# Two chained cross-attentions: the semantic product in 32-row tiles, with the Gram matrix's symmetry between token groups

## The chip, the cores and the metric

One core of a Trainium2 chip runs the kernel. Its engines are TensorE (PE in the profile, with PEld for its weight loads), VectorE (DVE), ScalarE (ACT), GpSimd (POOL) and SyncE (SP), whose queue issues nearly all DMAs here. The metric is the device time of one execution in microseconds (us). Each engine works through its own instructions in order; semaphores hold an instruction back until its inputs are there.

## The reference

64 batch elements of 256 queries and 320 channels, with a context of 77 tokens of 512 channels, pass through two cross-attentions, 20 heads of 16 channels each. The first layer is plain softmax attention over the 77 tokens (its image branch over an empty set of tokens gives nothing). The second, cut to what matters:

```python
text_ehs, ip_ehs = encoder_hidden_states[:, :-4], encoder_hidden_states[:, -4:]   # 73 and 4 tokens
probs_t = softmax(einsum('bhsd,bhtd->bhst', q, k_t) * attn_scale)
text_out = einsum('bhst,bhtd->bhsd', probs_t, v_t)
attn_scores = einsum('bhsd,bhnd->bhsn', q, k_ip) * attn_scale
qsem = l2norm(einsum('bhst,bte->bhse', probs_t, text_ehs))     # 512 channels, per head and query
sem = einsum('bhse,bne->bhsn', qsem, l2norm(ip_ehs))
probs_ip = softmax(attn_scores + 0.5 * sem) * spatial_mask
out = (text_out + einsum('bhsn,bhnd->bhsd', probs_ip, v_ip)) @ W_out + b_out + residual
```

`qsem` need not be built. With the Gram matrix G = ctx ctx^T of the 77 tokens, the dot product of an unnormalized qsem with an image token is the weight vector w times a column of G, and its squared norm is w^T G w. So one product of w with a matrix [G | values | ones] of 77 + 16 + 1 = 94 columns (GV) gives, per head and query: 73 columns whose weighted sum is the norm, 4 image scores, the 16 channels of the text output and the softmax's sum. This is the semantic product.

## The kernel before, in words

The batch is worked in pairs of elements (p, 32 pairs). A pair has ten units per layer (u = 0 to 4 for b = 0, then for b = 1); a unit is 128 rows of queries times 8 heads, laid out as 4 row quarters r by 2 heads e. The main loop has one step g per unit; step k = g mod 10 of a pair runs unit g of the first layer and, 13 steps later (LAG), the same unit of the second layer. Within a step PE runs, in this order: the semantic product of the second layer's unit of two steps ago (`semantics`), both layers' scores (`scores`, L659) into the same PSUM tile `sc`, the transposes of the second layer's weights (`transposed`, L723, L724), some of the projections, and the transposes of the first layer's. `sc` has one set of four banks, one for each quarter r, so the next step's product can begin only when DVE and ACT have read this one: DVE takes the maxima (`mx`, L677), subtracts (`w`, L679), multiplies the semantic columns with the weights (`weighted`, L792 and L795, into `prod`) and reduces them to the norm (`nrm`, L1130); ACT copies the 21 other columns out (`sums`, L1057). ACT takes the exponentials: L690 writes the first 64 tokens of a second-layer unit into `parts1` and L691 the other 9; both are turned by PE and copied by ACT to `pt1` and `pr1` (L730, L731). POOL normalizes the first layer's weights (`parts`, L710).

The 73 tokens are split into 64 (M) and a rest of 9 (R1). Two heads' 64 tokens stand on the 128 rows of `pt`: chunk i, half j. The product of the 64 takes tiles of 64 rows by 64 columns of the array; the rest of all eight heads stands on one chunk of 128 rows, 32 per quarter, in tiles of 32 rows by 64, and adds to 30 columns (GR) of each head (L781):

```python
for i in range(4):
    for j in range(2):                       # 64 rows of pt: one head's 64 tokens
        for c in halves_of(P):               # 64 queries
            matmul(ps[c, i % 2 * 2 + j, at : at + GV], pt[half_rows, i, c], gv[b][half_rows, part, i, :], ...)   # L774
```

What the product multiplies with lies in `gv` (the 64) and `gr` (the 9), once for each b. `gram` (L512 to L527; in step k = 0 for b = 0 of the pair before, in k = 5 for b = 1) computes G; ACT copies it out (L516, L517), POOL scales the columns (L518 to L520: image columns by the norms, the columns of the 9 by 2, since their transposed part is left out), SP copies the 64 rows to the lower half of the partitions (L521) and the 9 rows to eight places of `g_rest` (L525). `place_gram` (k = 1 and 8) lets POOL spread them into `gv` (L530) and `gr` (L534). The values of both layers come from `value_rows` (k = 6 and 8), which writes them to DRAM (`v_rows`, L394). `values` (k = 0 and 4 for the second layer, 9 and 2 for the first) loads them back (L406): the 64 rows twice into `vm`, the rest eight times into `vr` or `v_rest`; `place_values` (k = 2 and 8; first layer 0 and 3) puts them into `gv` (L435, L441) and `gr` (L449, L455) on POOL. `keys_by_head` (L376, POOL) spreads the keys into `kbd`, which the scores multiply with; those of the second layer's b = 0 follow `place_gram` in step k = 1 and are first used in step k = 3.

PE, ACT, DVE and POOL run in the order in which the program issues their instructions (`keep_order`). For SP the scheduler chooses, after the first steps: a DMA can be issued ahead of ones that the program names before it. A DMA that waits holds all that stand behind it on SP.

## Time and profile before

| what | value |
|---|---|
| time, median of 3 runs | 2474.22 us (2473.43 to 2474.65) |
| the profiled execution's own time | 2474.45 us |
| its span, first to last instruction | 2472.7 us |
| TensorE clock granted | 0.999 of full |
| from one semantic product to the next in the chain, 1026 to 1100 us | 6.0 to 9.0 us |
| DVE waits for scores (mx after L659) | 339.3 us, 221 times |
| PE waits for ACT sums before the product (L774) | 23.0 us in the page's group |
| mean DMA traffic | 53 GB/s, 150914 packets |

How to read it: an engine's busy share says little here, since records of PE overlap each other. A line of a group gives line, engine, operation, tiles written and read, shape and count, then busy time, mean time of one, and idle time before it with what ended it. In the timeline a line gives the start in us from the span's start, the length, and how many records are merged in it. A shape such as 64*64 is the part of PE's array in use (rows by columns), and 64x94 the moving operand (rows by columns).

### The profile page before, as it was taken

Reading aid. Unit: us, or ns where it says so; the run is one execution under the profiler, and the core shown is the slowest. Engines: PE = TensorE matmul, PEld = TensorE weight load, DVE = VectorE, ACT = ScalarE, POOL = GpSimd, SP = SyncE. Lnnn points to the kernel's source line nnn. Section 1 sums busy time; section 2 is a strip of 40 time slices with the busy share of each in tenths; the row PEclk is TensorE's granted clock in tenths of the full one; section 3 lists DMA queues with packets and bytes.
Section 4 is the critical chain, followed back from the end, with each engine's and each line's share of the span. In section 5 each row is a group of like instructions: output and inputs, shape, how many; then the busy total and the mean of one; then the engine's idle time right before and its main releaser. Section 6 shows DMA issues by size and latency. Waiting matters only on the chain.

```text
span 2472.7 us, 100470 instructions
## 1 busy us (share of the span) xinstructions
PE 2394.2 (97%) x41118; PEld 1847.9 (75%) x41118; DVE 1987.4 (80%) x3673; ACT 1482.2 (60%) x3767; POOL 1370.9 (55%) x3483
## 2 busy tenths in 40 slices
PE   7899999999999999999999999999999999999888
PEld 5677777777777777777777777777777777777676
DVE  3588788888888888888888888888888888888864
ACT  3466666666666666666665666665665666666543
POOL 2455565566555656555656555556555556555542
PEclk9999999999999999999999999999999999999999
DMA  6212111112111112111121211121211121211000
GB/s 173 75 30 57 50 52 47 56 53 58 52 57 41 54 54 59 52 52 51 47 59 56 62 45 48 46 60 56 62 44 48 47 59 56 61 39 39 26 23 25
DMA packets 150914, 131.83 MB, mean 53 GB/s; under 512 B 45432, under 2 KB 129144, under 8 KB 150456
## 3 DMA queue, kind: packets, MB, share of 16 engines
q1 hardware_dynamic: 149592, 124.27, 17.5%
q8 instruction: 325, 5.32, 0.9%
q10 hardware_dynamic: 864, 1.15, 0.2%
q14 instruction: 133, 1.09, 0.1%
HBM read 87.43 MB, written 33.91 MB: 49 GB/s over the span
## 4 chain that ended last, share of the span: by engine, by line
PE 76%; DVE 12%; ACT 3%; DMA 3%; POOL 2%; issue 1%; SPq 1%; DVEq 0%; POOLq 0%; ACTq 0%
PE tr L723 10%; PE sc L774 9%; PE o_ps L547 8%; PE q_ps L547 8%; PE sc L659 7%; DVE w L679 5%; PE v_ps L390 4%; PE sc L781 4%; PE o_ps L632 3%; DVE mx L677 3%; PE k_ps L345 3%; PE pv L809 2%; PE q_ps L557 2%; PE o_ps L557 2%; PE q_ps L575 2%; PE pv L814 2%
## 5 line engine op out<-in xcount | busy, mean ns | idle before, releaser
L677 DVE TENSOR_REDUCE mx<-sc 128x8 f32<-128x584 f32 (+1 forms) x640 | 496.6, 776 | 342.1 <-PE sc L659 339.3
L710 POOL TENSOR_TENSOR parts<-w,sm 128x512 f32<-128x512 f32 (+1 forms) x640 | 440.6, 709 | 437.1 <-DVE sm L706 144.2
L679 DVE TENSOR_TENSOR w<-sc,mx 128x616 f32<-128x616 f32 x640 | 511.8, 800 | 73.0 <-DVE mx L677 1.4
L723 PE MATMUL tr<-ident,parts 128*128 128x128 f32 x2560 | 407.5, 282 | 9.5 <-ACT pt L730 5.6
L730 ACT COPY pt<-tr 128x512 f32<-128x512 f32 x320 | 187.1, 585 | 323.8 <-PE tr L723 318.9
L723 PEld LDWEIGHTS tr<-ident,parts 128*128 128x128 f32 x2560 | 284.2, 140 | 128.6 <-issue 83.1
L687 ACT ACTIVATE w<-w 128x616 f32<-128x616 f32 x320 | 230.1, 719 | 143.7 <-DVE w L679 142.7
L774 PEld LDWEIGHTS sc<-gv,pt 64*64 64x64 f32 x10240 | 233.5, 133 | 105.6 <-ACT sums L1057 52.7
L774 PE MATMUL sc<-gv,pt 64*64 64x94 f32 x10240 | 277.9, 245 | 23.6 <-ACT sums L1057 23.0
L694 POOL COPY att<-w 128x32 f32<-128x32 f32 x320 | 67.0, 209 | 354.6 <-DVE w L679 350.8
L705 DVE TENSOR_REDUCE sm<-w 128x8 f32<-128x616 f32 x320 | 250.9, 784 | 13.9 <-ACT w L687 13.8
L659 PE MATMUL sc<-kbd,q 32*64 32x154 f32 x10240 | 247.7, 293 | 1.1 <-ACT q L602 1.0
L547 PE MATMUL q_ps<-x,wq 128*128 128x256 f32 x1024 | 232.9, 380 | 5.3 <-ACT kT L348 5.3
L547 PE MATMUL o_ps<-aT,wo 128*128 128x256 f32 x1024 | 231.8, 379 | 0.7 <-ACT aT L945 0.7
L1057 ACT COPY sums<-sc 128x168 f32<-128x168 f32 x320 | 96.2, 301 | 225.8 <-DVE prod L795 223.9
L1130 DVE TENSOR_REDUCE nrm<-prod 128x8 f32<-128x584 f32 x320 | 226.7, 709 | 0.3
L792 DVE TENSOR_TENSOR prod<-sc,parts 128x512 f32<-128x512 f32 x320 | 217.9, 681 | 2.8 <-PE sc L781 2.8
L547 PEld LDWEIGHTS q_ps<-x,wq 128*128 128x128 f32 x1024 | 189.2, 190 | 30.2 <-ACT kT L348 7.3
L547 PEld LDWEIGHTS o_ps<-aT,wo 128*128 128x128 f32 x1024 | 189.6, 190 | 24.4 <-ACT aT L945 1.1
L690 ACT ACTIVATE parts<-w 128x512 f32<-128x512 f32 x320 | 206.4, 645 | 0.0
L749 ACT COPY pt<-tr 128x512 f32<-128x512 f32 x256 | 150.3, 587 | 66.9 <-PE tr L723 65.5
L390 PE MATMUL v_ps<-wv,cf 128*128 128x320 f32 (+1 forms) x624 | 179.2, 433 | 0.0
(144 smaller groups left out, 4560.3 us busy)
## 6 DMA issues: line engine op xcount, KB each, us to landing
out_dram<-x SPq DMA_DIRECT2D x64, 256.0 KB
x<-in_x_dram SPq DMA_DIRECT2D x31, 512.0 KB
v_rows<-vs SPq DMA_DIRECT2D x38, 320.0 KB
vm<-v_rows SPq DMA_DIRECT2D x152, 80.0 KB
ct<-in_ctx_dram SPq DMA_DIRECT2D x32, 308.0 KB
cf<-in_ctx_dram SPq DMA_DIRECT2D x38, 256.0 KB
g_rest<-gram_rest SPq DMA_DIRECT2D x512, 0.5 KB
v_rest<-v_rows SPq DMA_DIRECT2D x448, 11.2 KB
```

The lines of the kernel that those rows point to most:

```text
L390: nc.tensor.matmul(ps[:n, :C], cfs[i][:, k, :n], wv[l][:, k, :], start=(k == 0), stop=(k == KE - 1))
L547: nc.tensor.matmul(ps[b][:, m, :], w[:, k, m * P : (m + 1) * P], main[:, k, b * S : (b + 1) * S], start=(k == 0 and m == 0), stop=False,)
L659: nc.tensor.matmul(ps[c, r, 2 * T * l : 2 * T * (l + 1)], tokens[rows, c], kbd[rows, part].rearrange("p e t -> p (e t)"), start=start, sto ...
L677: nc.vector.tensor_reduce(mx, sc[:, :, :, :nt], AX.X, ALU.max)
L679: nc.vector.tensor_tensor(w, sc, mx.unsqueeze(3).broadcast_to([P, 4, 2, T]), ALU.subtract)
L687: nc.scalar.activation(w, w, AF.Exp, scale=SCALE)
L705: nc.vector.tensor_reduce(sm, w, AX.X, ALU.add)
L710: nc.gpsimd.tensor_tensor(two[:, 8 * t0 : 8 * t1].rearrange("p (h t) -> p h t", h=8), w[:, :, t0:t1], sm.unsqueeze(2).broadcast_to([P, 8, ...
L723: nc.tensor.transpose(ps[:, i, :], flat[:, i * P : (i + 1) * P], ident)
L774: nc.tensor.matmul(ps[c, i % 2 * 2 + j, at : at + GV], pt[half_rows, i, c], gv[b][half_rows, part, i, :], start=start and i < 2, stop=False,)
L792: nc.vector.tensor_tensor(prod[:, :, :, :M], sm[:, :, :, :M], w[:, :4].rearrange("p (e a) j t -> p (a j) e t", e=2), ALU.mult)
L1130: nc.vector.tensor_reduce(eight(stats[q, b][2], u), prod, AX.X, ALU.add)
```

## The change

The 64 main tokens are split into two groups of 32 (h = 0, 1), so that the token groups are 32, 32 and 9. The weights are written in the order (e, h) by (r, t): each chunk i is one head e and one group h, with the four quarters r on 32 rows each. The product of the 64 then takes tiles of 32 rows by 64 columns, like the rest and the scores. For h = 0 it computes all 94 columns; for h = 1 only the 62 from the second group on, as the Gram matrix is symmetric: the block of the first group's rows and the second's columns is doubled (a new POOL instruction in `gram`), and its transposed block is left out, as is done with the rest already. `gv` holds, for each row quarter, only that quarter's heads. The Gram rows go to the four quarters by eight DMAs into a new tile `gq` instead of one; the second layer's values are loaded sorted by row quarter (runs of 32 channels), for which `v_rows` gets a copy of its last 64 channels, written by one more DMA; `place_values` is then two POOL instructions instead of 14, and `place_gram` two copies (one for each h) and the same product for the rest. The first layer's values are loaded as before, but `vm` and the new `vq` no longer share a buffer. PE, ACT, DVE and POOL keep their order otherwise; of SP's DMAs, one g_rest comes first, then the eight gq, then the other seven g_rest.

```diff
-    gv = [const.tile([P, 3, 4, GV], F32, tag=f"gv{b}", name=f"gv{b}") for b in range(2)]
+    gv = [const.tile([P, 2, 3, 2, GV], F32, tag=f"gv{b}", name=f"gv{b}") for b in range(2)]
     gr = [const.tile([P, 3, 2, GR], F32, tag=f"gr{b}", name=f"gr{b}") for b in range(2)]
     for b in range(2):
-        nc.vector.memset(gv[b][:, :, :, GV - 1 :], 1.0)
+        nc.vector.memset(gv[b].rearrange("p h i e n -> p (h i e) n")[:, :, GV - 1 :], 1.0)
         nc.vector.memset(gr[b], 0.0)
         nc.gpsimd.tensor_copy(
             gr[b][:, :, :, GR - 1 :], rest1.unsqueeze(1).unsqueeze(3).broadcast_to([P, 3, 2, 1])
...
     for t in vips:
         nc.vector.memset(t[HT * NIP :], 0.0)
-    v_rest = [const.tile([P, C], F32, tag=f"v_rest{b}", name=f"v_rest{b}") for b in range(2)]
+    gq = [const.tile([P, 2, T], F32, tag=f"gq{b}", name=f"gq{b}") for b in range(2)]
+    v_rest = [const.tile([P, 3, QR], F32, tag=f"v_rest{b}", name=f"v_rest{b}") for b in range(2)]
     g_rest = [const.tile([P, R0], F32, tag=f"g_rest{b}", name=f"g_rest{b}") for b in range(2)]
     for t in (*v_rest, *g_rest):
         nc.vector.memset(t, 0.0)
-    parts1 = [const.tile([P, 5, 2, M], F32, tag=f"parts1{i}", name=f"parts1{i}") for i in range(3)]
+    parts1 = [const.tile([P, 5, P], F32, tag=f"parts1{i}", name=f"parts1{i}") for i in range(3)]
     for t in parts1:
         nc.vector.memset(t[:, 4], 0.0)
...
             nc.tensor.matmul(ps[:n, :C], cfs[i][:, k, :n], wv[l][:, k, :], start=(k == 0), stop=(k == KE - 1))
         nc.scalar.copy(stage[i][:n, l, :], ps[:n, :C])
         if l:
-            v_rows[i] = dram.tile([P, 2, C], F32, tag="v_rows", name=f"v_rows{i}", bufs=8)
-            nc.sync.dma_start(v_rows[i][:n], stage[i][:n])
+            v_rows[i] = dram.tile([P, C + 3 * P], F32, tag="v_rows", name=f"v_rows{i}", bufs=8)
+            nc.sync.dma_start(v_rows[i][:n, : 2 * C], stage[i][:n].rearrange("p l c -> p (l c)"))
+            nc.sync.dma_start(v_rows[i][:n, 2 * C :], stage[i][:n, 1, 2 * P :])
             if (i + 2) * P < NB * T:
                 load_rows(i + 2)
-    def from_rows(to, l, p, b, t0, t1):
+    def pieces(p, b, t0, t1):
         r0 = (2 * p + b) * T
         at, end = r0 + t0, r0 + t1
         while at < end:
             i, r = divmod(at, P)
             n = min(P - r, end - at)
-            o = at - r0 - t0
-            nc.sync.dma_start(to[o : o + n, :], v_rows[i][r : r + n, l, :])
+            yield at - r0 - t0, n, v_rows[i][r : r + n]
             at += n
     v0s = {}
...
     def values(l, p, b):
-        nt = (T, TT)[l]
-        rem = nt - M
-        vm = small.tile([P, C], F32, tag="vm", name=f"vm{l}_{p}_{b}", bufs=1)
-        vr = v_rest[b] if l else small.tile([8 * rem, C], F32, tag="vr", name=f"vr{p}_{b}", bufs=1)
-        for e in range(2):
-            from_rows(vm[e * M : (e + 1) * M, :], l, p, b, 0, M)
-        for i in range(8):
-            r = i // 2 * QR + i % 2 * rem if l else i * rem
-            from_rows(vr[r : r + rem, :], l, p, b, M, nt)
+        if l:
+            vm = small.tile([P, 2, 3, QR], F32, tag="vq", name=f"vq{p}_{b}", bufs=1)
+            vr = v_rest[b]
+            by_quarter = lambda rows: rows[:, C:].rearrange("t (i r c) -> r t i c", i=3, r=4)
+            for h in range(2):
+                for o, n, rows in pieces(p, b, h * QR, (h + 1) * QR):
+                    for r in range(4):
+                        nc.sync.dma_start(vm[r * QR + o : r * QR + o + n, h], by_quarter(rows)[r])
+            for o, n, rows in pieces(p, b, M, TT):
+                for r in range(4):
+                    for e in range(2):
+                        at = r * QR + e * R1 + o
+                        nc.sync.dma_start(vr[at : at + n], by_quarter(rows)[r])
+        else:
+            vm = small.tile([P, C], F32, tag="vm", name=f"vm{l}_{p}_{b}", bufs=1)
+            vr = small.tile([8 * R0, C], F32, tag="vr", name=f"vr{p}_{b}", bufs=1)
+            for t0, t1, to, m, count in ((0, M, vm, M, 2), (M, T, vr, R0, 8)):
+                for i in range(count):
+                    for o, n, rows in pieces(p, b, t0, t1):
+                        nc.sync.dma_start(to[i * m + o : i * m + o + n, :], rows[:, :C])
         fetched[l] = (vm, vr)
     def place_values(l, p, b):
...
         rem = (T, TT)[l] - M
         vm, vr = fetched[l]
         if l:
-
-            for j in range(2):
-                rows = slice(j * M, (j + 1) * M)
-                for part in range(2):
-                    nc.gpsimd.tensor_copy(
-                        gv[b][rows, part, :, T : T + D].rearrange("p (e a) d -> p e a d", e=2),
-                        vm[rows, 8 * D * part : 8 * D * (part + 1)].rearrange(
-                            "p (a j e d) -> p j e a d", a=2, j=2, e=2
-                        )[:, j],
-                    )
-                nc.gpsimd.tensor_copy(
-                    gv[b][rows, 2, :, T : T + D].rearrange("p (e a) d -> p e a d", e=2),
-                    vm[rows, HT * D + j * QR : HT * D + (j + 1) * QR]
-                    .rearrange("p (e d) -> p e d", e=2).unsqueeze(2).broadcast_to([M, 2, 2, D]),
-                )
-            for r in range(4):
-                rows = slice(r * QR, (r + 1) * QR)
-                full = [QR, 2, 2, D]
-                nc.gpsimd.tensor_tensor(
-                    gr[b][rows, :2, :, T - M : T - M + D],
-                    vr[rows, : HT * D].rearrange("p (i r e d) -> p r i e d", i=2, r=4, e=2)[:, r],
-                    rest1[rows].unsqueeze(1).unsqueeze(3).broadcast_to(full), ALU.mult,
-                )
-                c0 = HT * D + r % 2 * QR
-                nc.gpsimd.tensor_tensor(
-                    gr[b][rows, 2, :, T - M : T - M + D], vr[rows, c0 : c0 + QR].rearrange("p (e d) -> p e d", e=2),
-                    rest1[rows].unsqueeze(2).broadcast_to([QR, 2, D]), ALU.mult,
-                )
+            nc.gpsimd.tensor_copy(
+                gv[b].rearrange("p h i e n -> p (h i) e n")[:, :, :, T : T + D],
+                vm.rearrange("p h i (e d) -> p (h i) e d", e=2),
+            )
+            nc.gpsimd.tensor_tensor(
+                gr[b][:, :, :, T - M : T - M + D], vr.rearrange("p i (e d) -> p i e d", e=2),
+                rest1.unsqueeze(1).unsqueeze(3).broadcast_to([P, 3, 2, D]), ALU.mult,
+            )
             return
         v0, vr0 = v0s[b] = (
             small.tile([P, H // 2, 2, D], F32, tag="v0", name=f"v0_{p}_{b}", bufs=2),
...
             mask = ip_mask[rows, heads].unsqueeze(2).broadcast_to([rows.stop - rows.start, m, D])
             nc.gpsimd.tensor_tensor(v, v, mask, ALU.mult)
-    grams = {}
-
     def gram(p, b):
...
         for k in range(KE):
             nc.tensor.matmul(ps[:TT, :T], ct[:, k, b, :TT], ct[:, k, b, :], start=(k == 0), stop=(k == KE - 1))
         r = rip[:TT, (2 * p + b) * NIP : (2 * p + b + 1) * NIP]
-        g = small.tile([P, T], F32, tag="gram", name=f"gram{p}_{b}", bufs=2)
+        g = small.tile([M, T], F32, tag="gram", name=f"gram{p}_{b}", bufs=2)
         rows = small.tile([TT, R0], F32, tag="gram_rest", name=f"gram_rest{p}_{b}", bufs=2)
         nc.scalar.copy(g[:M, :M], ps[:M, :M])
         nc.scalar.copy(rows, ps[:TT, M:T])
         nc.gpsimd.tensor_mul(rows[:, R1:], rows[:, R1:], r)
         nc.gpsimd.tensor_scalar_mul(g[:M, M:TT], rows[:M, :R1], 2.0)
         nc.gpsimd.tensor_copy(g[:M, TT:], rows[:M, R1:])
-        nc.sync.dma_start(g[M:, :], g[:M, :])
+        nc.gpsimd.tensor_scalar_mul(g[:QR, QR:M], g[:QR, QR:M], 2.0)
+        for r in range(4):
+            for h in range(2):
+                nc.sync.dma_start(gq[b][r * QR : (r + 1) * QR, h, h * QR :], g[h * QR : (h + 1) * QR, h * QR :])
         gx = g_rest[b]
         for i in range(8):
             r0 = i // 2 * QR + i % 2 * R1
             nc.sync.dma_start(gx[r0 : r0 + R1, :], rows[M:TT, :])
-        grams[b] = g
     def place_gram(b):
-        g, gx = grams[b], g_rest[b]
-        nc.gpsimd.tensor_copy(
-            gv[b][:, :, :, :T], g.unsqueeze(1).unsqueeze(1).broadcast_to([P, 3, 4, T])
-        )
+        gx = g_rest[b]
+        for h in range(2):
+            n = T - h * QR
+            nc.gpsimd.tensor_copy(
+                gv[b][:, h].rearrange("p i e n -> p (i e) n")[:, :, h * QR : T],
+                gq[b][:, h, h * QR :].unsqueeze(1).broadcast_to([P, 6, n]),
+            )
         full = [P, 3, 2, R0]
         nc.gpsimd.tensor_tensor(
             gr[b][:, :, :, :R0], gx.unsqueeze(1).unsqueeze(1).broadcast_to(full),
...
             nc.scalar.activation(w, w, AF.Exp, scale=SCALE)
             return
         two = ws[l] = parts1[g % 3]
-        nc.scalar.activation(two[:, :4].rearrange("p (e a) j t -> p (a j) e t", e=2), w[:, :, :, :M], AF.Exp, scale=SCALE)
+        nc.scalar.activation(mains(two), w[:, :, :, :M].rearrange("p r e (h t) -> p r e h t", h=2), AF.Exp, scale=SCALE)
         nc.scalar.activation(
             rests(two), w[:, :, :, M:TT], AF.Exp, scale=SCALE
         )
         nc.gpsimd.tensor_copy(eight(stats[p, b][0], u), w[:, :, :, TT:])
+    def mains(two):
+        return two[:, :4].rearrange("p (e h) (r t) -> p r e h t", e=2, r=4)
+
     def rests(two):
-        r = two[:, 4].rearrange("p j (a c) -> p (j a) c", c=QR)
+        r = two[:, 4].rearrange("p (r c) -> p r c", c=QR)
         return r[:, :, : 2 * R1].rearrange("p r (e t) -> p r e t", e=2)
     def normalize(g):
...
         n = P if l else 8 * R0
         part, s = UNITS[l][u]
-        flat = w.rearrange("p i j t -> p (i j t)") if l else w
+        flat = w.rearrange("p i t -> p (i t)") if l else w
         ps = ptr.tile([P, 4, P], F32, tag="tr", name=f"tr{l}_{p}_{b}{u}")
         pr = ptr.tile([P, 4, P], F32, tag="tr", name=f"rtr{l}_{p}_{b}{u}")
         for i in range(4):
...
         part, _ = UNITS[1][u]
         pt, rt = rows
         for i in range(4):
-            for j in range(2):
-                half_rows = slice(j * M, (j + 1) * M)
-                at = SEM0 + i // 2 * GV
+            e, h = divmod(i, 2)
+            at = slice(SEM0 + e * GV + h * QR, SEM0 + (e + 1) * GV)
+            for r in range(4):
+                quarter = slice(r * QR, (r + 1) * QR)
                 for c in halves_of(P):
                     nc.tensor.matmul(
-                        ps[c, i % 2 * 2 + j, at : at + GV], pt[half_rows, i, c], gv[b][half_rows, part, i, :],
-                        start=start and i < 2, stop=False,
+                        ps[c, r, at], pt[quarter, i, c], gv[b][quarter, h, part, e, h * QR :],
+                        start=start and i == 0, stop=False,
                     )
         for r in range(4):
             quarter = slice(r * QR, (r + 1) * QR)
...
         sm = by_block(ps)
         prod = sp.tile([P, 4, 2, TT], F32, tag="prod", name=f"prod{p}_{b}{u}", bufs=1)
         nc.vector.tensor_tensor(
-            prod[:, :, :, :M], sm[:, :, :, :M], w[:, :4].rearrange("p (e a) j t -> p (a j) e t", e=2), ALU.mult
+            *(t[:, :, :, :M].rearrange("p r e (h t) -> p r e h t", h=2) for t in (prod, sm)), mains(w), ALU.mult
         )
         nc.vector.tensor_tensor(prod[:, :, :, M:], sm[:, :, :, M:TT], rests(w), ALU.mult)
         return prod
```

## The prediction

> **What bounds the kernel now.** I read the page first (busy shares, chain), then the timeline of single steps on PE, then the other engines and SP around the lines that the change touches.
>
> ```profile
> PE 2394.2 (97%) x41118; PEld 1847.9 (75%) x41118; DVE 1987.4 (80%) x3673; ACT 1482.2 (60%) x3767; POOL 1370.9 (55%) x3483
> ...
> PE 76%; DVE 12%; ACT 3%; DMA 3%; POOL 2%; issue 1%; SPq 1%; DVEq 0%; POOLq 0%; ACTq 0%
> ...
> L774 PE MATMUL sc<-gv,pt 64*64 64x94 f32 x10240 | 277.9, 245 | 23.6 <-ACT sums L1057 23.0
> ```
>
> PE has three quarters of the chain, and L774, the changed product, is its second line. 10240 records are 320 units x 16 matmuls x 2: each fp32 matmul shows as two records (two passes). The group's 277.9 us over 10240 is 0.027 us a record, but that isn't what one costs. The timeline, asked for short stretches, shows why (start, length, form, how many have begun by the end of the stretch):
>
> ```profile
> 1010.42 0.31 PE L774 MATMUL sc<-gv,pt 64*64 64x94 f32 x4
> ...
> 1010.42 0.39 PE L774 MATMUL sc<-gv,pt 64*64 64x94 f32 x8
> ...
> 1010.42 0.48 PE L774 MATMUL sc<-gv,pt 64*64 64x94 f32 x12
> ...
> 1010.42 0.56 PE L774 MATMUL sc<-gv,pt 64*64 64x94 f32 x16
> ...
> 1011.23 0.31 PE L781 MATMUL sc<-gr,pr 32*64 32x60 f32 x8
> ...
> 1011.23 0.37 PE L781 MATMUL sc<-gr,pr 32*64 32x60 f32 x16
> 1011.39 0.34 PE L659 MATMUL sc<-kbd,q 32*64 32x154 f32 x8
> ```
>
> PE works in waves: one record for each tile of the array, all tiles at once. Four tiles of 64 rows, 94 columns: each further wave adds 0.08 us (0.31, 0.39, 0.48, 0.56). Eight tiles of 32 rows, 60 columns: 0.06 us (0.31 to 0.37). So a wave's price goes with its columns, and eight tiles cost no more than four.
>
> ```profile
> 1002.21 0.88 PE L774 MATMUL sc<-gv,pt 64*64 64x94 f32 x32 [0.70 <-ACT sums L1057]
> 1003.02 0.37 PE L781 MATMUL sc<-gr,pr 32*64 32x60 f32 x16
> 1003.18 0.76 PE L659 MATMUL sc<-kbd,q 32*64 32x154 f32 x32
> ...
> 1047.36 1.09 PE L557 MATMUL o_ps<-aT,wo 64*64 64x256 f32 x16
> 1048.27 0.83 PE L774 MATMUL sc<-gv,pt 64*64 64x94 f32 x32
> 1049.03 0.37 PE L781 MATMUL sc<-gr,pr 32*64 32x60 f32 x16
> 1049.19 0.76 PE L659 MATMUL sc<-kbd,q 32*64 32x154 f32 x32
> ```
>
> From the product to the scores is 0.97 us (1002.21 to 1003.18): eight waves of 0.08 = 0.64, then 0.12 for two waves of L781; the other 0.21 is two restarts of 0.05 (the first wave after a change of tile shape starts its second pass late) and 0.11 in which PE drains between 64-row and 32-row tiles. After L557, itself in 64*64 tiles, there is no restart before L774: 0.92 us (1048.27 to 1049.19).
>
> **The change part by part.** *PE, the product.* 32 matmuls a unit in tiles of 32 rows x 64 instead of 16: 64 records, eight waves again, but half of them of 62 columns, and L781 and L659 follow in the same tile shape. New sum: restart 0.05, four waves of 94 columns at 0.08 = 0.32, four of 62 at 0.06 (the 60-column row; were they no shorter, 0.08) = 0.24, L781 2 x 0.06 = 0.12: 0.73 against 0.97, so 0.25 us saved with unrounded waves. After L557 the drain of 0.11 moves in front of the product and a restart comes back: 0.92 against 0.83, 0.09 saved.
>
> The Trainium skill, page "TensorE: Matmul & The Clock Gate", section "Wait — 56ns, not 53.3ns?", speaks against the change: matmuls never start less than about 25 ns apart, however few their columns. By it the 64 records would take 64 x 0.025 = 1.6 us, some 0.8 more than now, or 250 us more in all (an estimate from that page). The rows come first: eight records of L781 begin in under 0.06 us, 7 ns apart, because they go to different tiles.
>
> *Which steps keep the saving.* Ten steps of one unit make a pair; there are 32 pairs. A step is bounded either by PE's own queue or by the loop DVE (L677 to L795), ACT sums L1057, then L774 again, since one set of PSUM banks serves all. The saving lies inside that loop too, so it counts in both kinds, with these exceptions, read from the timeline of 1027 to 1100 us:
> - Three of ten steps begin after L557 (1048.27 is one): 0.09 each.
> - In the step of 1085.09 the transpose behind the scores waits for ACT:
>
> ```profile
> 1085.09 0.88 PE L774 MATMUL sc<-gv,pt 64*64 64x94 f32 x32 [0.34 <-ACT sums L1057]
> ...
> 1086.34 0.28 ACT L691 ACTIVATE parts<-w 128x72 f32<-128x72 f32 x1
> ...
> 1086.76 0.66 PE L723 MATMUL tr<-ident,parts 128*128 128x128 f32 x4
> ```
>
> L691 ends at 1086.62, 0.14 before L723; an end releases PE some 0.05 later (1084.74+0.30 to 1085.09 for sums). 0.08 of the 0.25 is left.
> - In the step of 1033.80 DVE is the bound: four L617 (1034.99, 1.55 us) precede mx, sums ends at 1040.82, PE starts at 1040.99. 0.17 less 0.05 leaves 0.11.
> - The other five keep 0.25. In the two that DVE's loop bounds, mx waits 0.38 and 1.31 us for PE, so it can start earlier.
>
> A pair: 5 x 0.252 + 3 x 0.095 + 0.08 + 0.11 = 1.74 us; x 32 = **55.6 us**. If every exception failed: 320 x 0.252 = 80.6.
>
> *ACT and DVE* (L690, L792): the same 512 elements, inner runs of 32 instead of 64. DVE's L795 has runs of 9: from 72 to 512 elements 223 to 681 ns, 1.04 ns an element, so run length shows no price; L690 (512, 645 ns) against L687 (616 flat, 719) is 0.71 an element. I take 0; ends: 0 and 0.05 us a step in the two DVE-bound steps (3 us).
>
> *POOL.* Values: 14 instructions of 230 to 286 ns (3.50 us) become a copy of 192 elements and a product of 96. Copies run from 238 ns (64 elements) to 961 (924), so 0.35, and 0.34 from L449 and L455: 2.8 us less. The Gram copy of 924 becomes 462 and 270 (0.57 + 0.41, +0.02), and one tensor-scalar of 32 elements comes (0.25, by L519). 2.5 us x 64 off POOL. POOL is 2% of the chain: 0 taken.
>
> *SP.* Per batch element: seven more Gram DMAs, six more for main values (ten where a row tile is crossed), none more for the rest; 38 more writes of v_rows. The view of SP and POOL in one pair:
>
> ```profile
> 1039.36 0.84 SPq L525 DMA_DIRECT2D g_rest<-gram_rest  x1
> 1040.30 0.54 SPq L521 DMA_DIRECT2D gram<-gram  x1
> 1040.89 5.23 SPq L525 DMA_DIRECT2D g_rest<-gram_rest  x7
> ...
> 1049.58 0.96 POOL L530 COPY gv<-gram 128x924 f32<-128x924 f32 x1
> 1050.50 0.31 POOL L534 TENSOR_TENSOR gr<-g_rest,rest 128x78 f32<-128x78 f32 x1
> ```
>
> In the changed order one g_rest DMA comes first, then eight gq, then seven g_rest. A gq issue is between gram's 0.54 and g_rest's 0.75: 4.7 to 6.0 us instead of 0.6, so the last g_rest issue ends at 1050.2 to 1051.5 instead of 1046.12. Packets land some 0.8 later: L534 waits 0.4 to 1.8 us. Behind it on POOL stand four L376 (2.3 us); the last feeds the layer-1 scores, wanted about 1056.8 (0.26 into L659 at 1056.50), less 0.6 for a faster PE. They end at 1053.6 to 1054.9: 1.3 to 2.6 us of cover. It shrinks where SP comes late: in 12 of 32 pairs twelve value DMAs stand in front of this Gram. A value issue (32 rows x 3 runs) lies between 0.32 (45 rows of vm) and 0.70 (9 rows of 52 bytes); I take 0.5, by the 64-row vm (0.46 to 0.60), and SP is on time; at 0.70 it is 2 us late. Taken: 0.25 us in those 12 pairs, **3 us**. The other longer waits of SP lie behind waits it has already (ct waits for L512, 229.5 us in 29 times).
>
> *Sum.* The profiled execution took 2474.45 us (span 2472.7), 0.01% above the median 2474.22. 2474.45 - 55.6 + 3 = **2422 us**.
>
> **Rivals.**
> 1. *Narrow waves are no shorter* (the weight load sets the wave). Then four waves of 0.08 instead of 0.06: five steps keep 0.16, L557's 0.01, the two others 0.08 and 0.11: 1.03 x 32 = 33 us, **2441**. For it: the row of 0.06 is L781 alone. Against: L781's second wave, with L659's loads behind it, did take 0.06.
> 2. *All steps keep the whole saving* (no drain behind L557, ACT and DVE move along): **2394**. Against it, the gap at 1003.02 and L691.
> 3. *The Gram comes late* (the slower side). If SP's issues are all at the dear end and the lateness adds up, POOL holds kbd, and layer-1 scores wait in one step of every pair. It eats the gain where the wait passes 1.74 us a pair, about 4 us late; at 6 us late, 32 x 3.5 - 55.6, **2530**. Half-way, 0.3 to 1 us a pair: 2430 to 2450.
> 4. *Records are priced singly*, at today's 0.024 to 0.027: 32 more a unit, +0.8 us x 320 = 250 us, less 30: **about 2690**. Against it, the waves shown. A twin: PE's instruction stream can't follow 224 records in 0.95 us; today 160 pass in 1.7 us without a gap.
> 5. *The change doesn't do what it says*: the order of PE's stream shows 8 + 8 + 8 + 8 matmuls of 94, 62, 94, 62 columns, so this is out.
>
> **How the numbers follow.** Forecast 0.60, rival 1 0.10, rival 2 0.07, half-way lateness 0.08, rival 3 in full 0.07, rival 4 and its twin 0.06; no change 0.02. Faster by over 0.2% (5 us, about what a measurement can tell): 0.85; within 0.02; slower 0.13. The range takes in the forecast, rivals 1 and 2 and the half-way lateness: 2390 to 2455. The forecast's own is 2410 to 2432: a restart more or less (0.05 x 320 = 16) and the DVE term.
>
> **What would show it.** L773 in 20480 records with forms 94 and 62 in 32*64 tiles; from the first of them to the first score 0.72 us after 128-row tiles (0.97 before); after L557 a gap 0.1 longer; L723's wait on L691 grown by 0.1 to 0.2 in one step of ten; POOL about 160 us less busy and an idle time in front of the gr product that ends with a g_rest DMA. Wrong if a wave of 62 columns takes 0.08 or more, if the scores wait for kbd, or if PE pauses for nothing visible inside the product.

## The result, and the profile after

The changed kernel takes 2561.34 us (median of four runs, 2547.10 to 2569.50) against 2474.43 (2473.43 to 2475.50) on the same chip: 1.0345 times as long, 95% interval 1.0296 to 1.0394. It is slower by 87 us; 2422 was forecast, in a range of 2390 to 2455. The profiled execution took 2569.5 us (span 2567.8), at the slow end of its four runs. The page, in the rows that answer to those shown of before:

```profile
PE 2445.7 (95%) x51358; PEld 1902.3 (74%) x51358; DVE 1989.0 (77%) x3673; ACT 1485.2 (58%) x3767; POOL 1226.7 (48%) x2843
...
PE 60%; DVE 17%; SPq 9%; ACT 4%; POOL 4%; DMA 4%; issue 3%; DVEq 0%; POOLq 0%; ACTq 0%
...
L773 PE MATMUL sc<-gv,pt 32*64 32x94 f32 (+1 forms) x20480 | 318.0, 240 | 27.6 <-ACT sums L1056 26.9
L654 PE MATMUL sc<-kbd,q 32*64 32x154 f32 x10240 | 286.7, 300 | 46.4 <-POOL kbd L377 44.4
```

POOL is 144 us less busy (160 was worked out); DVE and ACT are as before (their re-ordered instructions, L791 and L685, have the same means as L792 and L690: 681 and 645 ns). Two things are new. SP's queue, 1% of the chain before, is 9%, and POOL and DMA have 3 points more together. And PE's product takes more busy time, not less: 318.0 us against 277.9. The waits name the first:

```profile
POOL gr L529 <- DMA g_rest<-gram_rest: 122.0, 30, 6.4
...
PEld sc L654 <- POOL kbd L377: 50.3, 21, 6.1
PE sc L654 <- POOL kbd L377: 44.4, 20, 5.8
```

Before, POOL waited 2.5 us in all for g_rest; now 122.0 us in 30 waits, about 4 us each, and 20 times the second layer's scores (l = 1 in the code, "layer-1 scores" in the prediction) wait for kbd behind it. One such pair, in the timelines of SP, POOL and PE (start, length, operation, in brackets the idle time before it and what ended it):

```profile
982.87 4.45 SPq L423 DMA_DIRECT2D vq<-v_rows  x8
987.42 2.73 SPq L428 DMA_DIRECT2D v_rest<-v_rows  x7
...
992.80 0.84 SPq L518 DMA_DIRECT2D g_rest<-gram_rest  x1
993.76 5.66 SPq L514 DMA_DIRECT2D gq<-gram  x8
999.47 5.88 SPq L518 DMA_DIRECT2D g_rest<-gram_rest  x7
```

```profile
988.26 0.28 POOL L511 TENSOR_SCALAR gram<-gram 32x32 f32<-32x32 f32 x1
...
1000.01 1.05 POOL L524 COPY gv<-gq 128x462 f32<-128x462 f32 x2 [1.87 <-DMA gq<-gram]
1006.45 0.32 POOL L529 TENSOR_TENSOR gr<-g_rest,rest 128x78 f32<-128x78 f32 x1 [5.39 <-DMA g_rest<-gram_rest]
1006.73 0.70 POOL L377 TENSOR_TENSOR kbd<-kT,head_mask 128x308 f32<-128x308 f32 x1
...
1008.45 0.44 POOL L377 TENSOR_TENSOR kbd<-kl,head_mask 128x154 f32<-128x154 f32 x1
```

```profile
1004.14 0.90 PE L773 MATMUL sc<-gv,pt 32*64 32x94 f32 x56
...
1008.94 0.82 PE L654 MATMUL sc<-kbd,q 32*64 32x154 f32 x16 [3.20 <-POOL kbd L377]
1009.69 1.11 PE L721 MATMUL tr<-ident,parts 128*128 128x128 f32 x4
```

SP starts the Gram's first load at 992.80, over 4 us after the Gram's rows are ready (POOL's last work on them, L511, ends at 988.54), because it is still issuing values and outputs; the quarter loads take 5.66 us, and POOL stands 5.39 us at L529 with the four L377 behind it. PE stands 3.20 us, and then L721 takes 1.11 us where the same row before was 0.66: the granted clock, by windows over this stretch (busy time of PE, PEld, DVE, ACT, POOL, then the clock), had fallen to half and came back by 1015.

```profile
1008.90:1012.00 3.10, 3.06 (x27) 1.94 (x29) 2.03 (x3) 1.09 (x3) 3.02 (x9) 0.50 0.52 136
...
1015.00:1018.00 3.00, 3.00 (x16) 2.54 (x14) 0.48 (x1) 1.40 (x5) 2.98 (x6) 1.00 0.17 27
```

Over the whole span the clock is 0.989.

The second is in the product. Counting how many records of L773 have begun by the end of ever longer stretches, as for the kernel before:

```profile
1004.14 0.34 PE L773 MATMUL sc<-gv,pt 32*64 32x94 f32 x8
...
1004.14 0.42 PE L773 MATMUL sc<-gv,pt 32*64 32x94 f32 x16
...
1004.14 0.47 PE L773 MATMUL sc<-gv,pt 32*64 32x94 f32 x23
...
1004.14 0.57 PE L773 MATMUL sc<-gv,pt 32*64 32x94 f32 x33
1004.14 0.73 PE L773 MATMUL sc<-gv,pt 32*64 32x94 f32 x37
1004.14 0.80 PE L773 MATMUL sc<-gv,pt 32*64 32x94 f32 x44
1004.14 0.88 PE L773 MATMUL sc<-gv,pt 32*64 32x94 f32 x53
```

The first 33 go as forecast: a wave of eight at 94 columns 0.08 us (0.34 to 0.42), one at 62 columns 0.05. Then, from 1004.55 on, the records start one or two in each 16.6 ns instead of one in 7 ns (the 31 behind the 33rd take 0.45 us, 14 ns each): the stretches of the lines x16 and x33 end at 1004.35 and 1004.50, 17 records in 0.15 us; those of the lines behind them end at 1004.60, .70 and .80, with 4, 7 and 9 records in 0.1 us each. They keep to that beat through L780 and into L654. In medians by unit, from the first product matmul: the first rest product comes at 0.684 us (0.811 before), the first score at 0.911 (0.973), the transposes at 1.689 (1.666). What the narrower waves won has been given back before the last score.

By steps (means over the 32 pairs of the ten steps of a pair, before and after): the step with L377's wait 8.73 and 11.07 us, the other nine 64.31 and 64.87. A pair is 73.04 and 75.94.

### The profile page after: what moved, and what is told of

Same layout as the page of the kernel before. It is cut to its first block, busy times and chain, and to the rows that moved or that the text cites. A ratio compares the mean times of both kernels' runs of the same rounds, so it can differ in the third digit from the quotient of the medians.

```text
span 2567.8 us, 121405 instructions
## 1 busy us (share of the span) xinstructions
PE 2445.7 (95%) x51358; PEld 1902.3 (74%) x51358; DVE 1989.0 (77%) x3673; ACT 1485.2 (58%) x3767; POOL 1226.7 (48%) x2843
## 3 DMA queue, kind: packets, MB, share of 16 engines
q8 instruction: 405, 6.64, 1.1%
q14 instruction: 136, 1.11, 0.1%
## 4 chain that ended last, share of the span: by engine, by line
PE 60%; DVE 17%; SPq 9%; ACT 4%; POOL 4%; DMA 4%; issue 3%; DVEq 0%; POOLq 0%; ACTq 0%
PE sc L773 8%; PE q_ps L542 8%; PE tr L721 7%; DVE w L674 6%; PE sc L654 6%; PE v_ps L391 4%; DVE mx L672 4%; PE o_ps L542 4%; SPq L514 4%; SPq L518 3%; PE k_ps L346 3%; PE q_ps L552 2%; DVE prod L791 2%; ACT w L682 2%; PE q_ps L570 2%
## 5 line engine op out<-in xcount | busy, mean ns | idle before, releaser
L721 PE MATMUL tr<-ident,parts 128*128 128x128 f32 x2560 | 414.0, 285 | 10.6 <-ACT pt L728 4.9
L721 PEld LDWEIGHTS tr<-ident,parts 128*128 128x128 f32 x2560 | 288.6, 142 | 132.1 <-issue 86.4
L773 PEld LDWEIGHTS sc<-gv,pt 32*64 32x64 f32 x20480 | 275.2, 131 | 133.7 <-issue 58.6
L773 PE MATMUL sc<-gv,pt 32*64 32x94 f32 (+1 forms) x20480 | 318.0, 240 | 27.6 <-ACT sums L1056 26.9
L654 PE MATMUL sc<-kbd,q 32*64 32x154 f32 x10240 | 286.7, 300 | 46.4 <-POOL kbd L377 44.4
L654 PEld LDWEIGHTS sc<-kbd,q 32*64 32x64 f32 x10240 | 184.8, 131 | 58.3 <-POOL kbd L377 50.3
L791 DVE TENSOR_TENSOR prod<-sc,parts 128x512 f32<-128x512 f32 x320 | 217.9, 681 | 2.9 <-PE sc L780 2.9
L685 ACT ACTIVATE parts<-w 128x512 f32<-128x512 f32 x320 | 206.5, 645 | 0.0
```

Source lines behind the costliest of these rows:

```text
L654: nc.tensor.matmul(ps[c, r, 2 * T * l : 2 * T * (l + 1)], tokens[rows, c], kbd[rows, part].rearrange("p e t -> p (e t)"), start=start, sto ...
L685: nc.scalar.activation(mains(two), w[:, :, :, :M].rearrange("p r e (h t) -> p r e h t", h=2), AF.Exp, scale=SCALE)
L721: nc.tensor.transpose(ps[:, i, :], flat[:, i * P : (i + 1) * P], ident)
L773: nc.tensor.matmul(ps[c, r, at], pt[quarter, i, c], gv[b][quarter, h, part, e, h * QR :], start=start and i == 0, stop=False,)
L791: nc.vector.tensor_tensor(*(t[:, :, :, :M].rearrange("p r e (h t) -> p r e h t", h=2) for t in (prod, sm)), mains(w), ALU.mult)
```

## The experiments

Times are medians (four runs or more, two for the last run without second groups), ratios against the kernel before on the same chip. Two causes are told apart: the late Gram, and the pace of the product's records.

**The Gram placed later.**

```
@@ fillers, k == 1
-            add(1, p - 1, place_gram, 0)
@@ fillers, k == 3, last
+            add(1, p - 1, place_gram, 0)
```

> The changed kernel with one move: the first output's Gram (its rows, the seven quarter loads and the rest loads) is placed at the end of step 3 of a pair in place of step 1, so GpSimd doesn't come to wait for the rest loads before it copies the keys by head. Theory A (the rest loads land 4.5 to 5.5 us after GpSimd wants them, GpSimd's key copies and the score matmuls stand behind that wait, once a pair): the step that grew from 8.73 to 11.07 us goes back to about 8.7, 32 x 2.3 = 75 us come back, and the clock's low stretches behind that idle time go with it; what is left above the kernel before is the semantic product itself, about 24 us: 2485 to 2505 us. Theory B (TensorE's product is the whole loss and the waits only shift): 2540 to 2570 us, with the steps of a pair still summing to about 75.9 us. Theory C (the product as predicted saves 0.25 us a unit and only the Gram's place spoilt it): 2415 to 2430 us.

Measured 2510.92 us, 1.0162 (1.0128 to 1.0197). POOL's wait for g_rest falls from 122.0 to 0.7 us, PE's for kbd behind POOL, 44.4 before the move, is gone; the clock is 0.997, the grown step 8.88 us. 50 us come back, of the 75 that theory A had, and 35 stay, where it had 10 to 30: A in kind, not in size. C is out: the product as it is does not pay even where the Gram is in time. Of the 35, 24 are in the steps (73.91 a pair against 73.16 in the same move made on the kernel before, below) and 8 ahead of them: the first product starts at 122.98 us in place of 115.36. In the chain ahead of that start SP's queue issues the first pair's loads without a pause from 88.5 to 107.3 us, the first layer's values come after them, kbd behind these on POOL, and PE stands 4.62 us until 118.37 for keys that ACT could copy only then. Why the move makes this later than in the changed kernel itself (117.58) stays open.

**The same move in the kernel before** (the same diff on the other kernel).

> The kernel before with the one move of the Gram-later kernel (the first output's Gram placed at the end of step 3 in place of step 1). If the place is neutral where SyncE is on time, as the waits of the kernel before say (2.5 us in all behind the rest loads): 2470 to 2480 us, and what the Gram-later kernel has over 2475 (36 us) is the product's. If the earlier place was itself a cost of the kernel before, up to 20 us faster.

Measured 2476.47 us, 1.0001 (0.9992 to 1.0010). The place is neutral where the Gram is in time.

**The kernel before with the changed one's loads** (the second write of the value rows is added too).

```
@@ gram
         nc.sync.dma_start(g[M:, :], g[:M, :])
+        for r in range(4):
+            for h in range(2):
+                if r or h:
+                    nc.sync.dma_start(gq[b][r * QR : (r + 1) * QR, h, h * QR :], g[h * QR : (h + 1) * QR, h * QR :])
...
@@ values, l == 1
+                    for q in range(3):
+                        nc.sync.dma_start(vq[q * QR + o : q * QR + o + n, h], by_quarter[q])
```

> The kernel before, with its own 64-row product, and the loads of the changed one added on SyncE's queue: the seven quarter loads of the Gram between the rows and the rest loads (into a tile that nothing reads), six quarter loads of the values for each pair and output, and the second write of the value rows. TensorE and the other engines do what they did. Theory A (a late queue is most of the loss): about 75 us slower than before, 2535 to 2560 us, with GpSimd's wait for the rest loads at about 4 to 5 us in each pair. Theory B (the product is the loss): no change, 2470 to 2480 us. If both carry it, between 2480 and 2535.

Measured 2750.25 us, 1.1112 (1.1087 to 1.1137): far more than theory A said. The product is the old one (first score at 0.973 us), nine steps are as before or within 0.5 us, and the one behind the Gram grows from 8.73 to 16.53. The waits of this run:

```profile
POOL gr L552 <- DMA g_rest<-gram_rest: 258.2, 32, 10.0
...
PE sc L677 <- POOL kbd L377: 181.3, 30, 11.8
```

So the loads alone make the Gram late and PE wait, with no change in the product. The size is not that of the changed kernel: here the old Gram copy and value loads are kept too, POOL is 142 us busier, and the clock over the span falls to 0.953. Which of these makes it 8 us a pair in place of 2.3 stays open; the next two runs give the sizes.

**Which loads make it late.** The changed kernel, once without most of the Gram's quarter loads, once without most of the values' (what isn't loaded stays zero, so neither computes everything).

```
@@ gram
-        for r in range(4):
-            for h in range(2):
-                nc.sync.dma_start(gq[b][r * QR : (r + 1) * QR, h, h * QR :], g[h * QR : (h + 1) * QR, h * QR :])
+        nc.sync.dma_start(gq[b][:QR, 0], g[:QR])
```

> The changed kernel (Gram placed in step 1, as the change has it) with one of the eight quarter loads of each Gram kept, the other seven left out (that part of the Gram stays zero): SyncE is rid of about 7 x 0.65 = 4.6 us ahead of the rest loads, twice a pair. Theory Q (the Gram comes late because of its own quarter loads): GpSimd's wait for the rest loads (122 us in all in the changed kernel) falls under 15 us, the grown step is back at 8.8 to 8.9 us, and 50 us come back as with the Gram placed later: 2505 to 2515 us. Theory V (the value loads before it make it late, and the quarter loads only fill what is left): the wait stays at half or more, 2530 us or more.

```
@@ values, l == 1
-                    for r in range(4):
-                        nc.sync.dma_start(vm[r * QR + o : r * QR + o + n, h], by_quarter(rows)[r])
+                    nc.sync.dma_start(vm[o : o + n, h], by_quarter(rows)[0])
```

> The changed kernel with the quarter loads of the values cut to a quarter of them (two or three in place of eight; that part of the values stays zero); the Gram's loads stay. SyncE is rid of about 6 x 0.45 = 2.7 us ahead of a Gram, twice a pair. Theory V: in most pairs SyncE came 1 to 5.3 us late to the Gram's first load, and most of that goes: GpSimd's wait for the rest loads falls from 122 to under 40 us and 35 to 50 us come back: 2510 to 2525 us. Theory Q: the wait falls by no more than a third, 2540 us or more. If the two add up without either deciding, each brings back about 25 us here.

Measured 2500.37 us (1.0098, 1.0083 to 1.0113) and 2504.94 us (1.0116, 1.0099 to 1.0132). The waits, first of the run without the Gram's quarter loads, then of the one without the values':

```profile
POOL gr L527 <- DMA g_rest<-gram_rest: 12.0, 8, 3.8
...
PE sc L652 <- POOL kbd L377: 1.3, 1, 1.3
```

```profile
POOL gr L529 <- DMA g_rest<-gram_rest: 81.5, 28, 5.7
...
PE sc L654 <- POOL kbd L378: 5.2, 5, 2.4
```

Both theories were framed wrongly: either half is enough, and the step behind the Gram is 8.99 us in both runs. The two groups do different things. In the changed kernel SP starts the first output's Gram loads more than 1 us after the rows are ready in 21 of 32 pairs; that is so in 23 without the Gram's quarter loads, but in 5 without the values' loads, as in the kernel before (5). So the values' loads make the start late, and the quarter loads make the loading long. With the values' loads gone POOL still waits 28 times, 2.9 us on average, but PE hardly feels it (5.2 us in all): most of a wait of that length is covered by the work between kbd and the scores. With both groups of loads it is 4 us on average, and what lies above the cover lands on PE. The first run is also the cleanest price of the rest: without the late Gram the change costs 24 us (2500.37 less 2476.41), and the late Gram 61 (2561.34 less 2500.37), of which 44.4 us is PE's idle time behind kbd. The other 17 are no more than what the clock could account for, 0.989 against 0.998 (0.9% of 2,560 us is 23, if PE set the pace all the time); that they do come from it wasn't shown.

**The product: columns or records.** These three runs, and the first two with wider records, change the Gram-later kernel; the two that leave records out leave out that part of the semantic scores.

```
@@ semantics: the second token group over all 94 columns (the added ones are zeros)
-            at = slice(SEM0 + e * GV + h * QR, SEM0 + (e + 1) * GV)
+            at = slice(SEM0 + e * GV, SEM0 + (e + 1) * GV)
...
-                        ps[c, r, at], pt[quarter, i, c], gv[b][quarter, h, part, e, h * QR :],
+                        ps[c, r, at], pt[quarter, i, c], gv[b][quarter, h, part, e, :],
```

> The Gram-later kernel with the second token group's product taken over all 94 columns in place of 62 (the 32 added columns are zeros, so the sums stay): half of the 128 narrow matmuls grow by a half, their number stays. Theory D (past the first 20 or so pairs, each load-and-multiply pair of TensorE issues 16.6 ns after the one before, whatever its columns): no more than 0.03 us a unit from first product matmul to the transposes, which stay at about 1.70 us, and 0 to 10 us in all. Theory W (time goes by columns, a wave of eight at 94 in place of 62): 8 waves of 0.011 to 0.018 us more, 0.09 to 0.14 us a unit, 320 units, 28 to 45 us more than the Gram-later kernel.

Measured 2521.19 us, 10.3 more than the Gram-later kernel (the runs of each spread over 12 to 17 us, so the sum is rough); the transposes at 1.717 us, 0.028 more. Half of the product's records grew by a half and it cost what theory D allows at most, and about a third or less of the 28 to 45 us that W asks. So the 32 columns that the Gram's symmetry saves are worth 10 us.

```
@@ semantics
             e, h = divmod(i, 2)
+            if i == 3:
+                continue
```

> The Gram-later kernel without the eight matmuls of the second half's second token group (that part of the semantic scores is left out; its loads, copies and the rest product stay): 16 fewer records of TensorE a unit, 8 load-and-multiply pairs by 2 that share a start. Theory D (16.6 ns a pair of issue): first product matmul to transposes falls from about 1.70 us by 8 x 16.6 = 0.13 us if 8 pairs go, by 0.27 us if the records count as 16 pairs; 42 to 85 us less in all, as far as TensorE sets the step. Theory W (columns): 2 waves of 0.055 us, 0.11 us a unit and 35 us.

Measured 2478.68 us, 32 less than the Gram-later kernel. The transposes come at 1.555 us, 0.134 earlier: 8.4 ns for each of 16 records, the first of theory D's two prices. By itself this run doesn't decide, since the columns go with the records and W's figures (0.11 us, 35 us) fit as well. The run before it does: there 32 columns on each of 32 records cost 0.028 us, and at that price the 62 columns of these 16 would be 0.027 of the 0.134 us. Leaving out both second groups (the condition `if h:` in its place):

> The Gram-later kernel without both halves' second token group: 32 product records a unit in place of 64, 80 in the stretch to the last score in place of 112, all of them 32x64 (that part of the semantic scores is left out). A second point on the price of a record: leaving out 16 records took 0.133 us. If each costs 8.3 ns, transposes fall to 1.69 - 0.27 = 1.42 us after the first product matmul; if the queue of pairs runs dry and refills at 16.6 ns a pair, to 1.69 - 0.13 - 0.27 = 1.29 us; if the scores' own columns (0.12 to 0.13 us a wave, 4 waves) are the next bound, it stops at about the product's two waves of 0.08 by two, 0.32, plus the rest product 0.16, scores 0.47 and 0.22 to the transposes: 1.2 us. In all 30 to 60 us less than the kernel without one group, as far as VectorE doesn't set the step: 2430 to 2460 us.

Measured 2439.95 us, the transposes at 1.331 us: 32 records fewer take 0.358 us less, the second 16 of them 14 ns each. None of the three numbers holds: it lies between the first two, and the price of a record is not constant, 8 to 14 ns. What does hold is the order of size: the columns in question move the stretch by 0.03 us, the records by 0.13 and 0.36.

**Fewer, wider records.**

```
@@ semantics
-                for c in halves_of(P):
-                    nc.tensor.matmul(
-                        ps[c, r, at], pt[quarter, i, c], gv[b][quarter, h, part, e, h * QR :],
+                nc.tensor.matmul(
+                    ps[:, r, at], pt[quarter, i, :], gv[b][quarter, h, part, e, h * QR :],
```

> The Gram-later kernel with each pair of 32x64 product matmuls (the two halves of the queries) made one of 32x128: the same columns and the same eight waves by columns, half the records (32 in place of 64 of the product a unit, 80 in place of 112 in the stretch to the last score). Theory D (from the first 50 or so records on, the stretch goes by its number of load-and-multiply records, at 8.3 to 16.6 ns each as the runs with full columns and without one group showed): 32 x 8.3 = 0.27 us a unit less, transposes at 1.40 to 1.45 us after the first product matmul in place of 1.69, and 320 x 0.25 = 80 us less where TensorE sets the step: 2430 to 2450 us, under the kernel before. Theory W (the weights' columns to load set the pace, a 128-wide record costs two of 64): 1.69 us stays, 2500 to 2515. Theory M (a change of tile shape between the product and the two 32x64 steps beside it costs a drain of about 0.1 us each time): 1.40 + 0.2 = 1.6 us, 2480 to 2500.

Measured 2549.57 us, 1.0299 (1.0282 to 1.0316): 39 us slower than the Gram-later kernel where D said 60 to 80 faster. The product's records in the timeline, by growing stretches:

```profile
900.23 0.36 PE L772 MATMUL sc<-gv,pt 32*128 32x94 f32 x4
900.23 0.47 PE L772 MATMUL sc<-gv,pt 32*128 32x94 f32 x8
900.23 0.56 PE L772 MATMUL sc<-gv,pt 32*128 32x94 f32 x12
900.23 0.67 PE L772 MATMUL sc<-gv,pt 32*128 32x94 f32 x16
900.23 0.81 PE L772 MATMUL sc<-gv,pt 32*128 32x94 f32 x20
900.23 0.92 PE L772 MATMUL sc<-gv,pt 32*128 32x94 f32 x24
```

A wave of four now takes 0.09 to 0.14, 0.11 us on average: the weight loads in the trace follow each other at 0.11 us at 94 and at 62 columns alike, so the 128 columns to load set the pace (theory W, for this shape), and the drain before L779 comes on top (first rest product at 1.048 us). None of the three forecasts holds: W for this shape names the right bound, but had 2500 to 2515 us. The run doesn't say what the records would do at this count, since another bound came first. With the rest product and the scores in 32x128 too:

> As the kernel with the product in 32x128 tiles, and the rest product and the scores in 32x128 tiles too: 56 records in the stretch in place of 112, one tile shape. Theory D: the records no longer set the pace and the columns do: product 4 x 0.08 + 4 x 0.055 = 0.54 us, rest product about 0.12, scores 4 x 0.12 = 0.48, and 0.22 to the transposes: 1.35 us in place of 1.69, 2400 to 2430 us. Theory W (columns of the weights to load): 1.69 us or more, 2500 us or more.

Measured 2530.58 us, 1.0223 (1.0208 to 1.0238): the drain is gone, the loads' 0.11 us a wave stays, the transposes are at 1.853 us, as W said (1.69 or more). And the kernel before with only its rest product and scores widened:

> The kernel before, its 64x64 product kept, with the rest product and the scores in 32x128 tiles in place of 32x64: half of their records. Theory D: the kernel before has 80 records in the stretch and only its last 24 or so start at 16.6 ns, so there is little to win: 0 to 0.1 us a unit from the first product matmul to the transposes (1.667 us before), 0 to 30 us. Theory W: no change or, with fewer tiles in flight, slower by up to 0.1 us a unit.

Measured 2499.52 us, 1.0095 (1.0080 to 1.0110), the transposes at 1.771 us in place of 1.666. D's "0 to 0.1 us less" is a miss, and W's "slower by up to 0.1 us" holds; the rest product's two waves cost 0.27 us to the first score in place of 0.16. The 64-wide halves are the better shape in both kernels.

**What sets the beat.** The changed trace holds a comparison, in another pair where the second layer's scores wait for kbd (timeline of PE around 704 us, the last line from a stretch ending at 707.83):

```profile
703.98 0.35 PE L780 MATMUL sc<-gr,pr 32*64 32x60 f32 x7
...
704.18 0.49 PE L654 MATMUL sc<-kbd,q 32*64 32x154 f32 x12
707.75 0.56 PE L654 MATMUL sc<-kbd,q 32*64 32x154 f32 x8 [3.08 <-POOL kbd L377]
```

The two lines of L654 have the same shape; each belongs to 16 records, the first shows the last twelve and the second the first eight. Those that come right behind the product start 16.6 ns apart (twelve in 704.18 to 704.38). Those that come after PE has stood 3 us start at 7 ns: eight in 0.05 us, then the next eight 0.26 us later (the granted clock was 0.50 there), again at 7 ns. So the spacing goes by what PE did just before. But these records have 154 columns, and in the kernel before a wave of eight of them takes 0.13 us (they begin at 1003.18, .32, .45 and .58), 16 ns a record too: for L654 the comparison shows a different order and not a lower rate. The lower rate is in the narrow records. L780 starts seven in 0.1 us here, the last five 16.6 ns apart, where the same line of the kernel before started sixteen in 0.15 us (L781 at 1003.02), and the product's own records, one line in one shape, go at 7 ns up to the 33rd and at 14 ns on average behind it.

The place of the break speaks against columns as well. By medians over the units it comes behind the 32nd or 33rd record in the changed kernel, in the run with all 94 columns, in the one with 16 records fewer and in the one with 32 fewer, where the 33rd is already one of the rest product; from the 36th on one or two start in each 17 ns. It is as if a stock of records, full after a wait, lets PE run at 7 ns, and once it is used up new ones come at 16.6 ns a load-and-multiply pair, sometimes two of a kind at a time. That the pace of the narrow records falls after 32 or 33, whatever their columns, is shown by these runs; the stock is an inference, and where in the machine it would lie is open. The instruction queue in the page's list of DMA queues moved 6.64 MB against 5.32, which fits fetched instructions as the source but doesn't prove it.

Of the runs that compute everything none is faster than the kernel before. The one without both second groups is (2439.95 us), at the price of what it leaves out.

## Why the prediction was wrong

*The sum for PE failed, and with it the forecast.* The step that failed reads "four waves of 94 columns at 0.08 = 0.32, four of 62 at 0.06 = 0.24, L781 2 x 0.06 = 0.12: 0.73 against 0.97, so 0.25 us saved". The prices of single waves were right: the first four waves took 0.08 and 0.05. What was missing was a second bound, the pace of many records in a row. It had been named, as the twin of rival 4 ("PE's instruction stream can't follow 224 records in 0.95 us; today 160 pass in 1.7 us without a gap"), and was given 6 in 100 with rival 4, on an argument that proves nothing: 160 records in 1.7 us (80 loads and 80 multiplies) is 21 ns a pair, slower than the 16.6 ns of the later beat, so the old stream could never show the limit on the whole. It showed it at one place that wasn't looked at, the last records of the scores, after sixteen of L781 and twenty-nine of L659 had gone at 7 ns within their waves. In the timeline of the kernel before, with stretches ending at 1003.60, .61, .62 and .64:

```profile
1003.18 0.71 PE L659 MATMUL sc<-kbd,q 32*64 32x154 f32 x28
1003.18 0.71 PE L659 MATMUL sc<-kbd,q 32*64 32x154 f32 x29
1003.18 0.73 PE L659 MATMUL sc<-kbd,q 32*64 32x154 f32 x30
1003.18 0.75 PE L659 MATMUL sc<-kbd,q 32*64 32x154 f32 x31
```

The last three of the wave come 12, 18 and 16 ns apart in place of 7. Why 45 records could go before it there, and 33 in the changed kernel, is open. The eight records of L781 "in under 0.06 us", the row the step leant on, were a burst; as evidence for 112 pairs in a row it was too short.

*The rule that was weighed and put aside* (the Trainium skill, "TensorE: Matmul & The Clock Gate", section "Wait — 56ns, not 53.3ns?") came nearer than the row in that many small records are bound by something other than their columns. Its size isn't seen here: by 25 ns the 64 records would have taken 1.6 us, and from the first product to the first rest product it is 0.68.

*The saving that would have remained after the bound*: first product to transposes is 0.023 us longer (0.252 shorter was taken), after L557 0.074 longer plus the drain that was forecast there (gap 0.196 to 0.307 us in front of the product, 0.11 as worked out). With the prediction's three steps behind L557, 10 x 0.023 + 3 x 0.051 + 3 x 0.11 = 0.71 us a pair, 23 us longer in place of 55.6 shorter; with the four that the trace has (123 of 320) it is 28. The run without the Gram's quarter loads measured 24. This is an estimate, as if PE set every step.

*The term for SP* ("SP is on time ... Taken: 0.25 us in those 12 pairs, 3 us") measured 61 us. Its single prices were nearly right: a quarter load 0.59 us in the median and eight in 5.66 in the pair shown (4.7 to 6.0 was given), a value load 0.42 (0.5 taken), the landing 1.1 after the last issue (1005.35 to 1006.45; 0.8 taken), the cover of 1.3 to 2.6 us nearly so, by the run in which 2.9 us did little harm. What failed is "SP is on time". SP issues 923 DMAs more over the kernel (3596 against 2673), 565 us of issue time or 17.7 us a pair. In the pair shown it came to the Gram's first load 4 us late, and over 1 us late in 21 of 32 pairs, where the prediction, at 0.5 us a load, had it on time; without the values' loads that lateness is gone in most pairs. It adds to the time of the quarter loads, and only the sum passes the cover. That is rival 3 ("if SP's issues are all at the dear end and the lateness adds up"), given 7 in 100; the lateness did add up, with issues at the middle of their range. It named place and chain rightly (POOL holds kbd, layer-1 scores wait, once a pair); its 3.5 us a pair at 6 us late stands against 2.3 us in that step at about 4.

*The clock* was in no term: PE's waits of 3 us and more came with stretches at half clock behind them (the one shown: 0.50).

*Right:* POOL's 160 us off (144), nothing on ACT and DVE, the order of PE's matmuls, the drain behind L557, and in the paragraph on what would make the prediction wrong the two that happened: scores that wait for kbd, and PE slowing for nothing visible inside the product.

## What to carry to other kernels

Price a split of matmuls by two bounds, columns per wave and records per microsecond, and take the second from the longest dense run of records in the trace, at its end, never from a burst of eight. When a change adds loads to a queue, add up the queue's issue time over the whole loop and see when it reaches each consumer; lateness that each of two additions alone would hide, both together put on the critical path. An edit that saves columns by making more tiles is worth what its columns cost at the new bound, and here that was 10 us of 2,500.

## What the hardware showed unasked

- Load-and-multiply pairs of fp32 tiles of 32x64 start 7 ns apart within their waves for the first 32 or 33 records of a product, then one or two in each 16.6 ns, 14 ns on average to the 64th, with 60, 62 and 94 columns alike.
- Tiles of 32x128 take 0.11 us a wave of four at 94 columns, against 0.08 in 64x64 tiles: there the weight loads follow each other at 0.11 us, at 62 columns too.
- After PE's wait of 3.2 us the granted clock was 0.50 for the next 3.1 us and 0.59 for the 3 after; the run with the longest waits (up to 11.8 us) had 0.953 over its span.
- SP's time for issuing one load went by its shape: 0.59 us for 32 rows of 308 or 180 bytes, 0.42 for 32 rows of 3 x 128, 0.70 for 9 rows of 52 (medians).
